# A Strassen-type factorization kernel: narrower column groups, and the sums of weight quadrants made by accumulating DMAs

## The chip, the cores and the metric

The kernel runs on one core of a Trainium2 chip. The core has five engines that run their own instruction queues side by side and meet only through semaphores: PE (matrix multiplication), DVE (vector operations), ACT (scalar engine: copies and squares here), POOL (GpSimd: elementwise additions here, and an issuer of DMAs) and SP (which only issues DMAs here). The metric is the device time of one execution in microseconds (us); lower is better.

## The reference

```python
out_lin = x @ lin_w.T + lin_b                                  # x: 1024 x 512, lin_w: 512 x 512
xv = jnp.einsum('bf,efm->bem', x, weight)                      # weight: 64 x 512 x 512
zp = jnp.einsum('bf,efm->bem', jnp.square(x), jnp.square(weight))
interaction = 0.5 * jnp.sum(jnp.square(xv) - zp, axis=1)
return out_lin + interaction
```

For each of 512 output columns m there are 64 embeddings e, so `xv` is a product of a 1024 x 512 matrix with a 512 x 32768 matrix, all in f32. Nearly all the work is there. `zp` needs no large product: summed over e it is `square(x)` times the sum over e of the squared weights, a 512 x 512 matrix called `w2_sum`.

## The kernel before, in words

**Two levels of Strassen's scheme.** The 32768 columns are done in 16 groups of 2048 (32 outputs of 64 embeddings). In each group x and the weight are cut into 2 x 2 quadrants, and seven products (outer products, numbered 1 to 7 in `ORDER = (1, 6, 2, 7, 4, 5, 3)`) stand in for eight. Each outer product is itself done in the same way, from seven inner products: that is `tree(s, g, i)` (line 416). An inner product is a "pair": two matmuls of 128 rows by 128 by 512 columns into the two banks of one PSUM buffer (`b1`, `b3`, or one of two `b2`). A group has 49 pairs, 98 matmuls; each f32 matmul shows as two records in the profile.

**The left operands.** X1 to X7, sums of quadrants of x, are built once in the beginning (lines 343 to 368), each with its seven inner sums, from x loaded into `oa0` to `oa3`.

**The right operands.** A group's weight quadrants w11, w12, w21, w22 are loaded by `load` (line 378), each in two halves of 1024 columns' worth named `.0` and `.1`. The outer sums are made in place or in T1 and T2 by `outer_sum` (line 384), all on DVE, two instructions each: T1 = w12 - w11, T2 = w22 - T1, w12 = w22 - w12, w21 = w21 - T2. The right operand of outer product i is named in `RHS` (line 412). Outer product 2 uses w21 as loaded, outer product 4 uses w21 after the last of these sums; one tree, 7, lies between them. The inner sums of each operand, `t` 1 to 4 with 512 columns, are POOL's (lines 420 to 427), in two buffers each.

**Evacuation.** Within a tree the products accumulate in PSUM: product 5 into b3, ACT copies it out as `p5`; product 3 is added into b3, ACT copies that as `p53`; product 1 into b1, ACT copies b1 into b2; 6, 7 and 4 add to b2, 2 adds to b1, and each of the four results is taken out after its product (`outer_psum` and `outer_sbuf`, lines 451 to 480) by DVE, with a second addition on DVE or POOL, into the outer results `oa`, `ob` and `c`. Finished results are squared on ACT and reduced over e on DVE (`finish`, line 402). `w_squares` does the same with the raw weights, for `w2_sum`. The buffers p5 are two, p53 three.

**The order.** All instructions are collected in a `Plan` (line 27) with costs for the engines that can do them, and `order` plays the program through on an event list: each engine takes, of what is ready, what is due first, with due times counted back from PE's sequence. Shared additions can go to DVE or POOL; DVE takes one only when it is due within 4 us (`spare`). PE's sequence itself is fixed: a product's key is 7 times the tree's number plus its place in

```python
PLACE = {5: -6, 3: -2, 1: 0, 6: 3, 2: 4, 7: 6, 4: 9}
```

so that neighbouring trees overlap: in the steady state PE runs 1, 5 of the next tree, 4 of the tree before, 6, 2, 3 of the next tree, 7, and so on. `pick` lets PE take nothing but the next product of that chain (lines 112 to 117). The order found is the static order of every engine's queue; at run time each engine waits for its semaphores in that order.

**Beginning and end.** A first stage computes `x @ lin_w.T + lin_b` (line 325) and parks it in DRAM; a last stage multiplies -0.5 square(x) by `w2_sum` (line 565), adds the parked parts and writes the output.

Of the kernel before, what the change touches and what calls it, by code (L numbers as in the profile page):

```python
# [17 lines left out]
G = 2  # L18
ORDER = (1, 6, 2, 7, 4, 5, 3)

SLOT = {1: 0, 7: 1, 2: 2, 4: 3, 5: 4, 6: 5, 3: 6}

PLACE = {5: -6, 3: -2, 1: 0, 6: 3, 2: 4, 7: 6, 4: 9}
# [3 lines left out]
class Plan:  # L27

# [33 lines left out]
    def order(self, spare=4.0):  # L62
# [6 lines left out]
        for o in reversed(ops):  # L69
            for d in o.deps:  # L70
                ops[d].succ.append(o.n)
        waiting = [len(o.succ) for o in ops]
        stack = [o for o in ops if not o.succ]
        while stack:
# [3 lines left out]
            for x in o.succ:  # L78
                latest = min(latest, ops[x].latest - cost)
# [11 lines left out]
        done, late, nxt = [], 0.0, 0  # L91
# [5 lines left out]
        def ready(o):  # L97
            return max([0.0] + [ops[d].end for d in o.deps]) + self.HOP
# [35 lines left out]
        while len(done) < len(ops):  # L134
            now = heapq.heappop(times)
            moved = True
            while moved:
                moved = False
                for e in pending:
# [6 lines left out]
                    if e == PE:  # L146
                        nxt += 1
# [25 lines left out]

@with_exitstack
def kernel(
# [8 lines left out]

    nc = tc.nc
    NG, NQ, _, NCB, KH, N = weight.shape
    B = xT.shape[1]
    M = out.shape[1]
    NB = B // P
    NK = 2 * KH
    MG = M // NG
    MI = MG // 4  # L210
    E = N // MI
    H = B // 2
    Q = B // 4

# [9 lines left out]

    buf = {}

    def make(name, shape, pool=sb):
        buf[name] = pool.tile(shape, F32, tag=name, name=name)
        return name

    def ring(tag, n, shape, pool=sb):
        names = [make(f"{tag}_{i}", shape, pool) for i in range(n)]
        state = [0]

        def take():
            state[0] += 1
            return names[(state[0] - 1) % n]
# [3 lines left out]
    half = [P, 2, N]  # L241
    for i in range(1, 8):
        make(f"X{i}", [P, 7, Q])
# [3 lines left out]
    for pos in range(4):  # L247
        make(f"oa{pos}", half)
        make(f"ob{pos}", half)
    t_ring = {k: ring(f"t{k}", 2, [P, N]) for k in range(1, 5)}  # L250
    p5_ring, p53_ring = ring("p5", 2, half), ring("p53", 3, half)
    c_ring, wsq_ring = ring("c", 3, half), ring("wsq", 2, half)
    make("b1", [P, G, N], ps)
    make("b3", [P, G, N], ps)
    b2_ring = ring("b2", 2, [P, G, N], ps)
    acc_ring = ring("acc", 2, [P, NB, MG])
    w2_sum = sb.tile([P, NK, M], F32, tag="w2_sum", name="w2_sum")
    bias = sb.tile([P, M], F32, tag="bias", name="bias_sb")
# [5 lines left out]
    PAIR = 1.72  # L264

    def two_input(o, a, b, sub, size=1024, psum=False):

        costs = {DVE: 0.08 + 1.06 * size / 1024}
        if not psum:
            costs[POOL] = 0.14 + 2.19 * size / 1024  # L270

        def emit(e):
            f = engines[e].tensor_sub if sub else engines[e].tensor_add
            f(o, a, b)  # L274

        return costs, emit

    def whole(o, a, b, sub=False, only=None, psum=False):

        costs, emit = two_input(buf[o], buf[a], buf[b], sub, psum=psum)  # L280
        plan.add({e: c for e, c in costs.items() if only in (None, e)}, emit, (a, b), (o,),
                 both=not psum)

    def act(o, i, func, reads, writes, cost=1.04):
        def emit(_):
            if func is None:
                nc.scalar.copy(o, i)  # L287
            else:
                nc.scalar.activation(o, i, func)  # L289

        plan.add({ACT: cost}, emit, reads, writes)

    def reduce(o, i, reads, writes):
        plan.add(
            {DVE: 1.14},
            lambda _: nc.vector.tensor_reduce(  # L296
                o, i.rearrange("p a (m e) -> p a m e", e=E), axis=AX.X, op=ALU.add
            ),
            reads, writes,
        )  # L300
# [3 lines left out]


    x_src = xT.rearrange("(p k) b -> p k b", k=NK)
    lw_src = lin_wT.rearrange("(p k) m -> p k m", k=NK)
    nc.gpsimd.dma_start(bias, lin_b.partition_broadcast(P))
    for k in range(NK):
        q, r = divmod(k, KH)  # L310
        for h in range(2):
            name = f"oa{2 * h + q}"
            dma(buf[name][:, r, :], x_src[:, k, ts(h, H)], (), ((name, r),),
                1.2, 2.0, nc.sync if h == 0 else nc.scalar)
        dma(buf[f"ob{q}"][:, r, :], lw_src[:, k, :], (), ((f"ob{q}", r),), 1.2, 2.0)

    lin_banks = ["b1", "b3", "b2_0", "b2_1"]
    for k in range(NK):
        q, r = divmod(k, KH)
        for g, bank in enumerate(lin_banks):  # L320
            h = g // 2

            def emit(_, k=k, q=q, r=r, g=g, h=h, bank=bank):
                for j in range(G):
                    nc.tensor.matmul(  # L325
                        buf[bank][:, j, :],
                        buf[f"oa{2 * h + q}"][:, r, ts((g * G + j) % (NB // 2), P)],
                        buf[f"ob{q}"][:, r, :],
                        start=(k == 0),
                        stop=(k == NK - 1),  # L330
                    )

            plan.add({PE: PAIR}, emit, ((f"oa{2 * h + q}", r), (f"ob{q}", r)),
                     (bank,), key=-1000 + 4 * k + g)
    for g, bank in enumerate(lin_banks):
        o = ("ob2", "ob3", "c_0", "c_1")[g]
        for j in range(G):
            costs, emit = two_input(buf[o][:, j, :], buf[bank][:, j, :], bias, False, 512, True)
            plan.add(costs, emit, (bank,), ((o, j),))
        dma(lin_dram[:, ts(g, G), :], buf[o], ((o, 0), (o, 1)), (o,))  # L340

    def block4(i):
        return buf[f"X{i}"][:, 0:4, :].rearrange("p (k q) b -> p k (q b)", k=2)

    a_buf = {"A11": "oa0", "A12": "oa1", "A21": "oa2", "A22": "oa3"}

    def a_parts(*names):
        return tuple((a_buf[n], r) for n in names if n in a_buf for r in range(KH)) + tuple(
            n for n in names if n not in a_buf
        )  # L350

    def a_ap(n):
        return buf[a_buf[n]] if n in a_buf else block4(int(n[1]))

    for i, n in ((1, "A11"), (2, "A12"), (4, "A22")):
        act(block4(i), a_ap(n), None, a_parts(n), (f"X{i}",))
    for i, a, b, sub in ((5, "A21", "A22", 0), (6, "X5", "A11", 1), (7, "A11", "A21", 1), (3, "A12", "X6", 1)):
        costs, emit = two_input(block4(i), a_ap(a), a_ap(b), sub)
        plan.add(costs, emit, a_parts(a, b), (f"X{i}",), both=True)
    for i in ORDER:  # L360
        x = buf[f"X{i}"]
        a11, a21, a12, a22 = (x[:, s, :] for s in range(4))
        s1, s2, s4 = (x[:, s, :] for s in range(4, 7))
        for o, a, b, sub in ((s1, a21, a22, 0), (s2, s1, a11, 1), (s4, a12, s2, 1), (a21, a11, a21, 1)):
            costs, emit = two_input(o, a, b, sub, 256)
            plan.add(costs, emit, (f"X{i}",), (f"X{i}",), both=True)
    for n in a_buf.values():
        plan.add({SP: 0.0}, None, (), (n,) + tuple((n, r) for r in range(KH)))
    for n in ("ob0", "ob1", "ob2", "ob3", "c_0", "c_1"):
        plan.add({SP: 0.0}, None, (), (n, (n, 0), (n, 1)))  # L370


    QUAD = ("w11", "w12", "w21", "w22")

    def w(g, q):
        return q + "ab"[g % 2] if q == "w22" else q

    def load(g):
        for q in (0, 1, 3, 2):
            for c in range(NCB):  # L380
                n = f"{w(g, QUAD[q])}.{c}"
                dma(buf[n], weight[g, q][:, c], (), (n,))

    def outer_sum(g, which):
        o, a, b = {
            1: ("T1", "w12", "w11"),
            2: ("T2", w(g, "w22"), "T1"),
            3: ("w12", w(g, "w22"), "w12"),
            4: ("w21", "w21", "T2"),
        }[which]  # L390
        for c in range(NCB):
            whole(f"{o}.{c}", f"{a}.{c}", f"{b}.{c}", True, DVE)

    def w_squares(g, q):
        row, col = divmod(QUAD.index(q), 2)
        for c in range(NCB):
            n, sq = f"{w(g, q)}.{c}", wsq_ring()
            act(buf[sq], buf[n], AF.Square, (n,), (sq,), 1.07)
            m = g * MG + (2 * col + c) * MI
            reduce(w2_sum[:, ts(row, KH), m:m + MI], buf[sq], (sq,), (("w2", row, m),))  # L400

    def finish(g, i, n, pos):
# [211 lines left out]
```

## Time and profile before

| | |
|---|---|
| median of 3 runs | 1438.88 us (1438.18 to 1439.22) |
| the profiled execution, first to last instruction | 1436.8 us |
| PE, time in matmul records | 1408.8 us, 98% |
| DVE | 1245.7 us, 87%, 1006 instructions |
| POOL | 1149.6 us, 80%, 691 instructions |
| ACT | 748.8 us, 52%, 756 instructions |
| bytes moved by DMA | 83.54 MB, a mean of 58 GB/s |

A line of the profile's groups or of its timeline names engine, source line, operation, output and inputs by the program's tile names, and the shape; `x4` is a count. "Busy" and "mean ns of one" are durations; what stands in brackets or behind a bar is the idle time of the engine just before, and who released it. PEld is the loading of the left operand into PE, which overlaps the matmul before. Most operations are recorded through one helper line, so that L274 is every addition on DVE or POOL, L287 every ACT copy, L289 every square, L296 every reduction, L438 every pair of a tree; they are told apart by tiles.

### The profile page before, as it was taken

The page shows a single profiled execution, that of the slowest core. Times are in us where ns is not written, and L with a number is a line of the kernel's source. Part 1 is how long each engine was busy: PE and PEld are TensorE (multiplying, and loading weights), DVE is VectorE, ACT ScalarE, POOL GpSimd, SP SyncE. Part 2 cuts the span into 40 slices and gives each one's busy share as a digit, 9 for nine tenths or more (in the row PEclk, how much of TensorE's full clock was granted, in tenths as well). Part 3 has the DMA queues.
Part 4 walks back from the last instruction along what each step waited for, and adds up shares of the span by engine and source line. Part 5 has one row for each costly group of instructions (what it writes and reads, how often), then busy time and mean ns, then how long its engine had stood idle before and what let it go on. Part 6 is the DMA issues. An engine that isn't in the chain of part 4 may idle for free.

```text
span 1436.8 us, 10763 instructions
## 1 busy us (share of the span) xinstructions
PE 1408.8 (98%) x3264; PEld 619.3 (43%) x3264; DVE 1245.7 (87%) x1006; ACT 748.8 (52%) x756; POOL 1149.6 (80%) x691
## 2 busy tenths in 40 slices
PE   7999999999999999999999999999999999999998
PEld 3444444444444444444444444444444444444443
DVE  1899898998989899898988989899898888989984
ACT  1465554645545465564556555465554546556441
POOL 6988886878878688896878888687887868889781
PEclk9999999999999999999999999999999999999999
DMA  5311111111111112111111111111111111210221
GB/s 212 117 60 58 48 59 33 59 48 59 59 42 51 33 59 62 46 58 33 59 48 58 59 48 59 33 59 48 58 59 45 53 32 57 60 52 22 88 74 59
DMA packets 40377, 83.54 MB, mean 58 GB/s; under 512 B 18240, under 2 KB 19264, under 8 KB 40320
## 3 DMA queue, kind: packets, MB, share of 16 engines
q1 hardware_dynamic: 39664, 81.54, 18.1%
q10 hardware_dynamic: 576, 1.05, 0.2%
q8 instruction: 27, 0.44, 0.1%
q14 instruction: 30, 0.25, 0.1%
q0 software_dynamic: 80, 0.26, 0.0%
HBM read 76.68 MB, written 6.16 MB: 58 GB/s over the span
## 4 chain that ended last, share of the span: by engine, by line
PE 90%; POOL 4%; DVE 2%; issue 1%; ACT 1%; DMA 1%; DVEq 0%; POOLq 0%; SPq 0%
PE b L438 86%; POOL oa L274 3%; PE b L325 2%; PE b L565 2%; ACT p L287 1%; POOL t L274 1%; DMA ob<-lin_wT 0%; DVE p L274 0%; DMA T1.1_83<-lind 0%; DVE ob L274 0%; DVE w11.1_73 L536 0%; DVE w21.0_76 L274 0%; DVE oa L274 0%; DVE acc L296 0%; DVE w11.0_72 L536 0%
## 5 line engine op out<-in xcount | busy, mean ns | idle before, releaser
L438 PE MATMUL b<-t,X 128*128 128x512 f32 x1792 | 806.2, 592 | 2.0 <-DVE p L274 1.6
L438 PEld LDWEIGHTS b<-t,X 128*128 128x128 f32 x1792 | 340.0, 190 | 431.9 <-issue 415.0
L287 ACT COPY p<-b 128x1024 f32<-128x1024 f32 x224 | 225.6, 1007 | 266.1 <-PE b L438 226.8
L289 ACT ACTIVATE oa<-oa 128x1024 f32<-128x1024 f32 x128 | 131.9, 1054 | 165.3 <-DVE oa L274 90.9
L296 DVE TENSOR_REDUCE w_sum<-wsq 128x16 f32<-128x1024 f32 x128 | 154.8, 1211 | 29.0 <-ACT wsq L289 28.9
L287 ACT COPY b<-b 128x1024 f32<-128x1024 f32 x112 | 111.8, 998 | 91.1 <-PE b L438 85.2
L274 DVE TENSOR_TENSOR p<-b,p 128x1024 f32<-128x1024 f32 x96 | 117.0, 1218 | 43.4 <-PE b L438 43.4
L296 DVE TENSOR_REDUCE acc<-oa 128x16 f32<-128x1024 f32 x128 | 152.0, 1207 | 0.0
L438 PE MATMUL b<-w21.0_76,X 128*128 128x512 f32 x256 | 120.3, 592 | 0.0
L274 POOL TENSOR_TENSOR oa<-oa,p 128x1024 f32<-128x1024 f32 x32 | 102.8, 3212 | 1.8
L289 ACT ACTIVATE c<-c 128x1024 f32<-128x1024 f32 x64 | 67.7, 1058 | 67.8 <-DVE c L274 67.8
L274 POOL TENSOR_TENSOR oa<-p,oa 128x1024 f32<-128x1024 f32 x32 | 75.7, 2365 | 27.2 <-DVE p L274 26.9
L274 DVE TENSOR_TENSOR oa<-b,p 128x1024 f32<-128x1024 f32 x64 | 78.0, 1219 | 11.7 <-PE b L438 10.8
L274 POOL TENSOR_TENSOR c<-c,oa 128x1024 f32<-128x1024 f32 x32 | 75.4, 2357 | 13.8 <-DVE c L274 11.7
L274 POOL TENSOR_TENSOR oa<-oa,ob 128x1024 f32<-128x1024 f32 x32 | 76.4, 2387 | 6.9 <-DVE oa L274 6.9
L274 POOL TENSOR_TENSOR ob<-ob,oa 128x1024 f32<-128x1024 f32 x32 | 76.3, 2384 | 5.5 <-DVE ob L274 5.5
L274 POOL TENSOR_TENSOR t<-w21.0_76,t 128x512 f32<-128x512 f32 x32 | 40.8, 1275 | 48.3 <-PE b L438 48.3
L274 POOL TENSOR_TENSOR ob<-p,ob 128x1024 f32<-128x1024 f32 x32 | 75.7, 2364 | 0.5 <-DVE p L274 0.5
L296 DVE TENSOR_REDUCE acc<-ob 128x16 f32<-128x1024 f32 x64 | 75.9, 1209 | 0.0
L296 DVE TENSOR_REDUCE acc<-c 128x16 f32<-128x1024 f32 x64 | 74.8, 1208 | 1.1 <-ACT c L289 1.1
L438 PEld LDWEIGHTS b<-w21.0_76,X 128*128 128x128 f32 x256 | 48.6, 190 | 61.2 <-issue 61.2
L274 DVE TENSOR_TENSOR ob<-b,oa 128x1024 f32<-128x1024 f32 x32 | 39.1, 1223 | 40.5 <-PE b L438 39.8
(127 smaller groups left out, 2295.9 us busy)
## 6 DMA issues: line engine op xcount, KB each, us to landing
w11.0_72<-weight SPq DMA_DIRECT2D x16, 512.0 KB, 3.7
w11.1_73<-weight SPq DMA_DIRECT2D x16, 512.0 KB, 3.8
w12.0_74<-weight SPq DMA_DIRECT2D x16, 512.0 KB, 3.8
w12.1_75<-weight SPq DMA_DIRECT2D x16, 512.0 KB, 3.8
w21.0_76<-weight SPq DMA_DIRECT2D x16, 512.0 KB, 3.8
w21.1_77<-weight SPq DMA_DIRECT2D x16, 512.0 KB, 4.7
w22a.0_78<-weight SPq DMA_DIRECT2D x8, 512.0 KB, 3.8
w22a.1_79<-weight SPq DMA_DIRECT2D x8, 512.0 KB, 3.8
```

Source lines behind the costliest of these rows:

```text
L274: f(o, a, b)
L287: nc.scalar.copy(o, i)
L289: nc.scalar.activation(o, i, func)
L296: lambda _: nc.vector.tensor_reduce(o, i.rearrange("p a (m e) -> p a m e", e=E), axis=AX.X, op=ALU.add),
L325: nc.tensor.matmul(buf[bank][:, j, :], buf[f"oa{2 * h + q}"][:, r, ts((g * G + j) % (NB // 2), P)], buf[f"ob{q}"][:, r, :], start=(k == 0) ...
L438: nc.tensor.matmul(buf[b][:, j, :], buf[f"X{i}"][:, SLOT[p], ts(j, P)], op, start=first, stop=True, skip_group_check=True,)
L565: nc.tensor.matmul(buf[bank][:, j, :], buf[xe[h, k // KH]][:, k % KH, ts((g * G + j) % (NB // 2), P)], w2_sum[:, k, :], start=(k == 0), st ...
```

## The change

**Groups.** The 512 outputs are done in two groups of 16 and 20 groups of 24 (1024 and 1536 columns). A matmul has 256 columns in the first two groups and 384 in the others, where it had 512; there are 22 x 98 matmuls in trees where there were 16 x 98. Each operation on PSUM or SBUF shrinks alike, from 1024 elements per partition to 512 or 768.

**Outer sums.** They become four accumulating DMAs a group, issued from POOL, each over a whole quadrant: T1 is loaded with w12 and w11 is added from DRAM; T2 is loaded with w22 and T1 is added; w22 is added to w12 and T2 to w21, both in place. Minus signs are moved to the x side (X5, X6, X7, X3). T1 has two buffers, so that there are four more load instructions a group than before: T1 and T2 are loaded too.

**Order.** PE may take any product that is ready, the one with the smallest key first, as long as it is due within 20 us (`AHEAD`); the key is a time now, and never smaller than that of a product it depends on. Dependencies are kept for pieces of 128 elements of a tile instead of whole tiles. `spare` becomes 15 us.

**Buffers.** The inner sums t of a tree share one buffer, of which there are three (there were two of each); p53 has two instead of three; `c` is one buffer of the whole result.

A second kind of tree (`wide_tree`, `widen`, `HSLOT`, `HSEQ`) is in the source as well, but `HK` is empty and none of it is executed. It is left out here.

```diff
+HK = ()
+TBUF = 3
+SPARE = 15.0
+AHEAD = 20.0
+def groups(n_m):
+    return [16, 16] + [24] * ((n_m - 32) // 24)
...
         op.deps.discard(op.n)
+        op.after = max((self.ops[d].after for d in op.deps), default=-1e9)
+        if key is not None:
+            op.key = op.after = max(key, op.after + 1e-6)
...
-                if nxt < len(chain):
-                    o = chain[nxt]
-                    if not left[o.n] and ready(o) <= now + 1e-6:
-                        return o
-                return None
+                able = [n for n in pending[e]
+                        if ops[n].latest < now - late + AHEAD and ready(ops[n]) <= now + 1e-6]
+                return ops[min(able, key=lambda n: ops[n].key)] if able else None
...
-    for q in ("w11", "w12", "w21", "w22a", "w22b", "T1", "T2"):
-        for c in range(NCB):
-            make(f"{q}.{c}", half)
+    for q in ("w11", "w12", "w21", "w22a", "w22b", "T1a", "T1b", "T2"):
+        make(q, KH * WIDE)
...
-    p5_ring, p53_ring = ring("p5", 2, half), ring("p53", 3, half)
+    t_ring = ring([make(f"t{k}", 12 * V) for k in range(TBUF)])
+    p5_ring = ring([make(f"p5_{k}", WIDE) for k in range(2)])
+    p53_ring = ring([make(f"p53_{k}", WIDE) for k in range(2)])
...
+    def dma_add(o, i, rows, reads, writes):
+        token = ("token", len(plan.ops))
+        def emit(_):
+            nc.gpsimd.dma_start(o, i, accum_op=ALU.add)
+        cost = 2.9 * rows / 1024
+        plan.add({POOL: 1.0}, emit, reads + writes, writes + (token,), land=cost + 2.5)
+        plan.add({SP: cost}, None, (token,), ())
...
-    for i, a, b, sub in ((5, "A21", "A22", 0), (6, "X5", "A11", 1), (7, "A11", "A21", 1), (3, "A12", "X6", 1)):
+    tt(x_block(5), x_in(1, 1), x_in(1, 0), True)
+    minus_both(x_block(6), x_block(5), x_in(0, 0))
+    tt(x_block(7), x_in(0, 0), x_in(1, 0), True)
+    minus_both(x_block(3), x_in(0, 1), x_block(6))
...
     def outer_sum(g, which):
-        o, a, b = {
-            1: ("T1", "w12", "w11"),
-            2: ("T2", w(g, "w22"), "T1"),
-            3: ("w12", w(g, "w22"), "w12"),
-            4: ("w21", "w21", "T2"),
+        o, i = {
+            1: (w(g, "T1"), None), 2: ("T2", w(g, "T1")), 3: ("w12", w(g, "w22")), 4: ("w21", "T2"),
         }[which]
-        for c in range(NCB):
-            whole(f"{o}.{c}", f"{a}.{c}", f"{b}.{c}", True, DVE)
+        n = KH * GROUPS[g] // 2 * E
+        o = reg(o, 0, n)
+        if i is None:
+            dma_add(o.ap, source(g, 0), n, (), o.atoms)
+        else:
+            dma_add(o.ap, reg(i, 0, n).ap, n, reg(i, 0, n).atoms, o.atoms)
...
-            plan.add({PE: PAIR}, emit, (name, f"X{i}", b), (b,), key=7 * s + PLACE[p])
+        pair = 2 * mm_cost(n)
+        def product(p, bank, first):
+            mm([reg(bank, j * N, n) for j in range(2)],
+               [reg(f"X{i}", SLOT[p] * Q + j * P, P) for j in range(2)],
+               rhs[p], first, time + PLACE[p] * pair)
...
-        load(g)
+        load(g, (("w11", 0), ("w12", 1), (w(g, "T1"), 1), ("T2", 3)))
         outer_sum(g, 1)
         outer_sum(g, 2)
+        load(g, ((w(g, "w22"), 3), ("w21", 2)))
         w_squares(g, "w12")
```

The function `minus_both(o, a, b)` writes -a - b and runs on DVE only; `reg` names a piece of a tile; `source(g, q)` is the part of the weight in DRAM that belongs to quadrant q of group g.

More of the change, by code (lines that the diff above doesn't have):

```diff
@@ L90, in order @@
         times = [self.HOP]
[L91 removed]
+        done, late = [], 0.0
         def release(o):
@@ L97, in ready @@
         def ready(o):
-            return max([0.0] + [ops[d].end for d in o.deps]) + self.HOP
+            return max([0.0] + [d.end for d in o.waits]) + self.HOP
         def longer(e, by):
@@ L171, in order, with __init__, ap @@
         return done
+class Reg:
+    def __init__(self, tile, off, n, *outer):
+        self.tile, self.off, self.n, self.outer = tile, off, n, outer
+        self.size = n
+        offs = [off]
+        for step, count in outer:
+            self.size *= count
+            offs = [o + step * k for o in offs for k in range(count)]
+        unit = tile.unit
+        self.atoms = tuple(sorted({
+            (tile.name, a) for o in offs for a in range(o // unit, (o + n - 1) // unit + 1)
+        }))
+    @property
+    def ap(self):
+        t = self.tile.ap
+        free = [list(x) for x in self.outer] + [[1, self.n]]
+        return bass.AP(tensor=t.tensor, offset=t.offset + self.off, ap=[list(t.ap[0])] + free)
 @with_exitstack
@@ L272, in emit @@
         def emit(e):
             f = engines[e].tensor_sub if sub else engines[e].tensor_add
[L274 to L284, printed above, removed]
+            f(o.ap, a.ap, b.ap)
+        plan.add({e: c for e, c in costs.items() if only in (None, e)}, emit,
+                 a.atoms + b.atoms, o.atoms, both=not psum)
@@ L337 @@
[L337 to L349, printed above, removed]
-        )
@@ L352, in a_ap @@
[L352 to L356, printed above, removed]
-    for i, a, b, sub in ((5, "A21", "A22", 0), (6, "X5", "A11", 1), (7, "A11", "A21", 1), (3, "A12", "X6", 1)):
-        costs, emit = two_input(block4(i), a_ap(a), a_ap(b), sub)
-        plan.add(costs, emit, a_parts(a, b), (f"X{i}",), both=True)
+        name, off = ("c", g * 2 * M) if g < 3 else ("w22b", 0)
@@ new lines, with source, load @@
+    base = [0]
+    for mg in GROUPS:
+        base.append(base[-1] + mg)
+    def source(g, q):
+        iw = GROUPS[g] // 2 * E
+        lo = base[g] * F * E + q * P * KH * iw
+        return weight[lo:lo + P * KH * iw].rearrange("(p x) -> p x", p=P)
+    def load(g, names):
+        iw = GROUPS[g] // 2 * E
+        for name, q in names:
+            for k in range(KH):
+                o = reg(name, k * iw, iw)
+                dma(o.ap, source(g, q)[:, k * iw:(k + 1) * iw], (), o.atoms, 2.4 * iw / 1024)
```

552 lines of the change are left out of this document (362 added, 190 removed).

## The prediction

> **What bounds the kernel now.** I read the page first, for how full each engine is.
>
> ```profile
> span 1436.8 us, 10763 instructions
> PE 1408.8 (98%) x3264; PEld 619.3 (43%) x3264; DVE 1245.7 (87%) x1006; ACT 748.8 (52%) x756; POOL 1149.6 (80%) x691
> PEclk9999999999999999999999999999999999999999
> L438 PEld LDWEIGHTS b<-t,X 128*128 128x128 f32 x1792 | 340.0, 190 | 431.9 <-issue 415.0
> ```
>
> The PE is the bound, at full clock; no other engine is. What can be won is what the PE loses, so next comes its ideal pitch, from the timeline of the last stage, where nothing makes it wait, and of the cold start:
>
> ```profile
> 8.88 0.34 PEld L325 LDWEIGHTS b<-ob,oa 128*128 128x128 f32 x1 [0.52 <-issue]
> 13.15 0.28 PEld L325 LDWEIGHTS b<-ob,oa 128*128 128x128 f32 x1 [0.52 <-issue]
> ...
> 1404.47 1.88 PE L565 MATMUL b<-w_sum,w11.0_72 128*128 128x512 f32 x4
> ...
> 1430.22 1.88 PE L565 MATMUL b<-w_sum,w12.1_75 128*128 128x512 f32 x4
> ```
>
> Between the last two rows start 15 times 4 = 60 matmul records: 25.75/60 = 0.4292 us each (one matmul of the code is two records, a "product" on two halves is four). Cold, five records take 4.27 us, 0.854 each; half of that is 0.427, so some 0.0022 us a record doesn't shrink with the clock. The chain of waits gives the rest:
>
> ```profile
> 7.90 30.40 PE b L325 x64
> ...
> 288.04 3.30 POOL oa L274
> 291.38 0.94 issue
> 292.32 1.00 ACT p L287
> ...
> 373.24 3.29 POOL oa L274
> ...
> 1432.14 0.69 DVE w22a.1_79 L274
> ```
>
> A group repeats every 373.24-288.04 = 85.20 us; its 196 records need 196 x 0.4292 = 84.12. So 1.08 us a group is lost, 17.3 in 16 groups. The whole: 1432.14-7.90 = 1424.2, less 3264 x 0.4292 = 1400.9, less 30.40 - 64 x 0.4292 = 2.9 for the cold clock, leaves 20.4 us: 17.3 at the group turns, some 3 at the first and the last tree. The list of waits names the place, and the timeline at one turn the cause:
>
> ```profile
> PE b L438 <- ACT p L287: 13.4, 16, 1.1
> PE b L438 <- DVE p L274: 1.6, 2, 1.4
> ```
>
> ```profile
> 114.74 1.78 DVE L274 TENSOR_TENSOR T1.0_82<-w12.0_74,w11.0_72 128x1024 f32<-128x1024 f32 x1
> 116.44 2.28 DVE L274 TENSOR_TENSOR ob<-ob,p 128x1024 f32<-128x1024 f32 x1
> 117.60 3.33 POOL L274 TENSOR_TENSOR oa<-oa,p 128x1024 f32<-128x1024 f32 x1
> 118.64 3.36 DVE L274 TENSOR_TENSOR T2.0_84<-w22b.0_80,T1.0_82 128x1024 f32<-128x1024 f32 x1
> 121.92 0.99 ACT L287 COPY p<-b 128x1024 f32<-128x1024 f32 x1
> 122.97 1.55 PE L438 MATMUL b<-w11.1_73,X 128*128 128x512 f32 x3 [0.83 <-ACT p L287]
> ```
>
> DVE's outer sums T1 and T2 of the next group run side by side with POOL's last use of the buffer p of tree 5; both stretch (3.33 us, where the rows below have 2.37 for that size). p comes free late, the copy into it is late, product 3 of tree 1 waits.
>
> **The change part by part.** The instructions get shorter. These rows give two sizes for each kind, or one:
>
> ```profile
> L274 DVE TENSOR_TENSOR T2.0_84<-b,w21.0_76 x2: 677/678/680, 1412.0 to 1412.6; 128x512 f32<-128x512 f32 x2
> ```
>
> ```profile
> L274 DVE TENSOR_TENSOR p<-b,p 128x1024 f32<-128x1024 f32 x96 | 117.0, 1218 | 43.4 <-PE b L438 43.4
> L287 ACT COPY p<-b 128x1024 f32<-128x1024 f32 x224 | 225.6, 1007 | 266.1 <-PE b L438 226.8
> L274 POOL TENSOR_TENSOR oa<-p,oa 128x1024 f32<-128x1024 f32 x32 | 75.7, 2365 | 27.2 <-DVE p L274 26.9 <-POOL t L274 0.3
> L274 POOL TENSOR_TENSOR t<-w21.0_76,t 128x512 f32<-128x512 f32 x32 | 40.8, 1275 | 48.3 <-PE b L438 48.3
> ```
>
> *Columns.* Two groups with matmuls of 256 columns and 20 with 384 stream the same 1,605,632 columns as 16 x 196 records of 512, in 22 x 196 = 4312 records, 1176 more. At 0.0022 us that is +2.6 us; the lower bound is 0 (all of the pitch goes with the columns). Above: the weight load of 190 ns lies under a record of 216 ns at 256 columns and of 322 at 384, so hidden; were it a pitch of 0.23, the 392 small records would cost 5.5 us more. I take 2.6. A product takes 4 x 0.3222 = 1.29 us in a large group, 0.863 in a small one.
>
> *Outer sums off DVE.* DVE loses 8 instructions a group (T1.0 1.78, T2.0 3.36, w21.0 2.02 below among them), and with them the jam at the turn: -17.3. Linear between the rows, a 768-element DVE operation takes 0.95 us, POOL's 1.82, POOL's 384 sum 1.00. A large group has 63.1 us of PE work; DVE has 28 evacuations and 24 reductions, 52 x 0.95 = 49; POOL 28 sums t, 28, up to 14 shared additions, 25, and four DMA issues, which the nearest row puts at 0.68 each, 3: 56. Both fit, and DVE may take shared additions from POOL. So the ordinary windows should hold: the pair of products that hides an evacuation lasts 2.58 us against 0.2 (159.12 to 159.32 below) + 0.95 + 0.05 (the copy's end at 122.91 to 122.97) = 1.20.
>
> *What is late next.* The addition of T2 to w21 must come after tree 2 has used the raw w21 and before tree 4's first sum t. Before, that looks so:
>
> ```profile
> 149.58 1.22 DVE L274 TENSOR_TENSOR w21.1_77<-w21.1_77,T2.1_85 128x1024 f32<-128x1024 f32 x1
> ...
> 157.41 1.88 PE L438 MATMUL b<-w21.0_76,X 128*128 128x512 f32 x4
> 159.12 1.88 PE L438 MATMUL b<-w12.1_75,X 128*128 128x512 f32 x4
> 159.32 1.22 DVE L274 TENSOR_TENSOR oa<-b,oa 128x1024 f32<-128x1024 f32 x1 [0.42 <-PE b L438]
> 160.47 2.02 DVE L274 TENSOR_TENSOR w21.0_76<-w21.0_76,T2.0_84 128x1024 f32<-128x1024 f32 x1
> ...
> 162.57 1.28 POOL L274 TENSOR_TENSOR t<-w21.1_77,w21.0_76 128x512 f32<-128x512 f32 x1 [1.16 <-DVE w21.0_76 L274]
> ...
> 164.27 4.03 PE L438 MATMUL b<-t,X 128*128 128x512 f32 x9
> ```
>
> One half was added early, the other after product 2 (streamed until 159.12), and product 5 of tree 4 began 5.15 us later, just in time: three products lie between. In the changed kernel one accumulating DMA adds all of w21 after that product 2, and three products are 3.87 us. How long it takes is not in the trace; the nearest rows are plain transfers:
>
> ```profile
> 1.25 0.68 POOL L308 DMA_DIRECT2D bias_sb<-lin_b  x1 [0.80 <-POOLq L603]
> ```
>
> ```profile
> w11.0_72<-weight SPq DMA_DIRECT2D x16, 512.0 KB, 3.7
> accd<-acc SPq DMA_DIRECT2D x15, 128.0 KB, 2.4
> ```
>
> 1.3 us for 384 KB more gives 2.0 + 2.6 = 4.6 us for 768 KB, the lower bound; if every byte is handled twice (source and old destination), 2.0 + 5.2 = 7.2; two whole transfers in a row, 9.2, are the upper bound. I take 6, between the first two. Product 5 is then ready 0.2 (to POOL) + 0.5 (half of a POOL sum in the way) + 6 + 0.1 + 1.0 (t) + 0.1 = 7.9 us after product 2. Until then the new order lets PE go on: 3, 7, 1, 4, 6, 2, 7 of trees 2 and 7 are free, 7 x 1.29 = 9.03 us; the eighth, product 4 of tree 7, must wait for the evacuation ahead of it. So the DMA is hidden, with 1.1 us to spare. It costs nonetheless: with tree 4 left out, one product instead of two covers each evacuation, 1.29 against 1.20, and any DVE operation in the way shows. I allow a third of one, 0.3 us in each of 20 groups, 6 us (bounds 0 and 0.95 x 20 = 19). In the small groups the same count gives 6.2 against 6.04 us, and 0.93 against 0.863 for each evacuation: 1 us each, 2.
>
> *The rest.* Four more loads a group and the other three accumulations have 15 us and more between free and due (T2 is free after the addition to w21, three trees before the turn, and due a tree later); behind a DMA that waits on POOL's queue stand sums t and shared additions, and the third t buffer covers a tree, 9 us. Preparing X is due sooner, since small trees take 6.0 us, and now has two steps for DVE alone. All x has landed here:
>
> ```profile
> 18.51 1.04 ACT L287 COPY X<-oa 128x1024 f32<-128x1024 f32 x1 [5.47 <-DMA oa<-xT]
> ```
>
> From there to the first product (7.90 + 30.40 = 38.3) are 20 us; 28 steps of 256 columns at 0.41 (the DVE line) and four of 1024 at 1.22 are 16.4 on DVE alone, which no longer has T1 and T2 there: 0, and a few us if that cover fails. The last stage can fill the last tree's 1.4 us wait: -1.
>
> Sum against the profiled execution: 1436.8 - 17.3 + 2.6 + 6 + 2 - 1 = 1429.1; the median of the runs lies 2.1 above that execution's span: **1431 us**.
>
> **Rivals.** *The accumulation is late (slower).* Place: product 5 of tree 4, once a group. Each us over 9.03 - 1.9 = 7.1 is paid 20 times; it outweighs the gain from about 7.5 us a DMA (0.39 x 20 = the 7.7 us won). At 8.2, between the two upper bounds, 1.07 x 20 = 21.4, and 1 more in each small group: 1429.1 + 21.4 + 2 + 2.1 = 1455; at 9.2, 1477. For it: the source and destination must both be read, and the whole addition sits in one DMA. Against: few bytes are on the way,
>
> ```profile
> q1 hardware_dynamic: 39664, 81.54, 18.1%
> ```
>
> and nothing else becomes free to load at that point.
>
> The Trainium skill (TensorE: Matmul & The Clock Gate, "Why this matters for your kernels") says that PE gaps of over about 3 us bring the half clock back. The cold rows above show that clock, and no wait in this trace is long enough to show its return; by that rule a DMA of over 10 us would cost up to 2.9 us more a group, as the cold start did.
>
> *POOL can't issue in time (slower).* The turn above shows DVE and POOL stretching each other; if an issue is held up likewise, by a two-input DVE operation of 2.3 us, product 5 is ready at 10.2, 1.2 late: 1429.1 + 24 + 2.1 = 1455 as well. Against: without outer sums few DVE operations have both inputs in SBUF. The Trainium skill (SBUF — State Buffer, "Who interferes with whom") describes POOL-issued DMAs starved of descriptors by DVE, but for DVE's two-port modes, and infers that two-input additions don't do it; no run here shows an accumulating issue.
>
> *The wait only moves (no change).* With 0.7 instead of 0.3 us a group lost behind single covers, 1431 + 8 = 1439. For it: slack of 0.09 us; against: DVE has 20% left.
>
> *Nothing waits.* Without the 8 us allowed, 1423. Against: the same 0.09.
>
> **How the numbers follow.** Forecast 0.42 (own range 1424 to 1436); nothing waits 0.10; the wait moves 0.12; the accumulation late 0.28; the issue late 0.08. About 0.2% (2.9 us) is what a measurement can tell from no change: faster 0.52, same 0.12, slower 0.36. Range: from 1421, the forecast without any lost time and without the extra records, to 1465, which takes in the late cases up to a DMA of 8.7 us.
>
> **What would show it.** Right: no wait of product 3 on a copy at the turn; no T1, T2 sums on DVE; w21's accumulation landing within 7 us and PE running through it; groups repeating every 63.1 to 63.7 us. Wrong: PE waiting on POOL's t of tree 4; a POOL DMA issue of over 2 us; records of 256 columns apart by more than 0.22 us; new waits on DVE evacuations of over 0.7 us a group.

## The result, and the profile after

| | before | after |
|---|---|---|
| median | 1438.66 us (16 runs, 1438.18 to 1439.22) | 1442.9 us (16 runs, 1436.66 to 1447.37) |
| ratio to before, 95% interval | | 1.0029 [1.0016, 1.0042] |
| profiled execution | 1436.8 us | 1444.8 us |

The changed kernel is slower by 0.3%, where faster by 0.5% was forecast. What stands out besides is the spread: 1 us before, 10.7 us after. The page of the changed kernel, busy times:

```profile
PE 1422.6 (98%) x4440; PEld 839.8 (58%) x4440; DVE 1101.6 (76%) x1226; ACT 786.4 (54%) x1038; POOL 1149.3 (80%) x995
```

DVE has lost 144 us, as planned, and PE is still the bound. Where it loses time, the chain of waits of the changed kernel tells (start, duration, what):

```profile
6.12 26.97 PE b L369 x56
...
34.41 5.15 DVE X L391
...
102.59 7.95 DMA w<-T
...
117.75 8.50 DMA T<-T1a
...
168.28 60.94 PE b L335 x188
...
230.18 0.94 DVE acc L314
231.12 0.87 DVE oa L289
232.04 60.94 PE b L335 x188
...
701.01 5.91 DVE ob L289
...
1320.00 84.42 PE b L335 x260
...
1407.86 5.16 PE b L335 x16
...
1416.45 1.29 PE b L335 x4
...
1421.17 1.29 PE b L335 x4
```

Four places can be read off. **Regular groups** repeat every 232.04 - 168.28 = 63.76 us; 196 records at 0.3225 us (the twelve that start between 217.41 and 221.28 us) are 63.21, so 0.55 us is lost in each, 11 us in 20. **One event**: from 168.28 to 1320.00 are 18 periods, 1147.7 us, and 4.0 us more; they lie around 701. **The start**: 18 x 196 records and the last 284 leave 500 of 4312 ahead of 168.28, 392 of 256 columns (0.2158 us each) and 108 of 384: 119.4 us. The first stage's 64 records, begun at 6.12, take 64 x 0.4292 and 2.9 us more for the cold clock, and end at 36.5; 131.8 us were taken from there, so 12.4 us are lost before the groups become regular. **The end** loses 0.6 us: 284 x 0.3225 + 64 x 0.4292 = 119.1 of the 119.7 us from 1320.00 to the end of the last matmul at 1439.67.

The timeline of the changed kernel in two of these places, the start and the second narrow group:

```profile
25.77 0.88 POOL L325 DMA_DIRECT2D T<-T1a  x1 [2.13 <-DMA T1a<-weight]
...
34.33 5.24 DVE L391 SCALAR_TENSOR_TENSOR X<-oa,X 128x1024 f32<-128x1024 f32 x1
...
110.68 2.05 PE L335 MATMUL b<-w,X 128*128 128x256 f32 x4 [2.04 <-DMA w<-T]
```

At 25.77 POOL's queue had stood still for 2.13 us behind an accumulation that waits for T1a. All that POOL had to do then came in one gapless stretch, and the addition for X3 on DVE, whose two inputs are both in SBUF, took 5.24 us, where it takes 1.74 in E3 below. At 110.68 the accumulation into w21 was late itself, and the product after the gap took 2.05 us in place of 1.03.

The event around 701 us, with the same place one group later below it:

```profile
684.10 0.86 POOL L325 DMA_DIRECT2D T<-T1b  x1 [0.95 <-DMA T<-weight]
...
700.38 1.92 POOL L289 TENSOR_TENSOR oa<-oa,p 128x768 f32<-128x768 f32 x1
...
701.01 5.90 DVE L289 TENSOR_TENSOR ob<-ob,p 128x768 f32<-128x768 f32 x1
702.15 1.11 POOL L289 TENSOR_TENSOR t<-w,t 128x384 f32<-128x384 f32 x1
...
703.10 1.10 POOL L289 TENSOR_TENSOR t<-T,t 128x384 f32<-128x384 f32 x1
...
704.06 1.09 POOL L289 TENSOR_TENSOR t<-T 128x384 f32<-128x384 f32 x1
...
705.01 1.08 POOL L289 TENSOR_TENSOR t<-w,t 128x384 f32<-128x384 f32 x1
...
707.86 2.93 PE L335 MATMUL b<-w,X 128*128 128x384 f32 x4 [2.17 <-ACT p L299]
...
768.26 1.81 POOL L289 TENSOR_TENSOR oa<-oa,p 128x768 f32<-128x768 f32 x1 [0.27 <-DVE p L289]
...
768.89 2.00 DVE L289 TENSOR_TENSOR ob<-ob,p 128x768 f32<-128x768 f32 x1
...
770.03 1.72 POOL L289 TENSOR_TENSOR t<-w,t 128x384 f32<-128x384 f32 x1
```

A load of T came late (5.8 us from issue to landing, 4.4 one group later), POOL stood 0.95 us behind the accumulation that waits for it, and from there on POOL has no time to spare: its instructions overlap, the next starts 0.14 us and more before the one ahead has ended (702.15 against 700.38 + 1.92). DVE's addition, dispatched in the midst of them, ends only after POOL has run dry at 706.1. Then p is late, the copy is late, PE waits 2.17 us. One group later POOL isn't pressed: its next instruction starts only 0.04 us before the end of the one ahead (770.03 against 768.26 + 1.81), DVE gets in after that one, and the POOL instruction is the one that waits (1.72). In the other regular groups POOL waited at this place for 0 to 0.53 us, and the addition took 2.0 us.

And what the prediction asked first, how long an accumulation takes (kilobytes each, median us from issue to landing, changed kernel):

```profile
w<-T POOLq DMA_DIRECT2D x20, 768.0 KB, 6.0
...
T1a<-weight POOLq DMA_DIRECT2D x10, 768.0 KB, 7.0
...
T1b<-weight POOLq DMA_DIRECT2D x10, 768.0 KB, 8.5
```

### The profile page after: what moved, and what is told of

Same layout as the page of the kernel before. It is cut to its first block, busy times and chain, and to the rows that moved or that the text cites. A ratio compares the mean times of both kernels' runs of the same rounds, so it can differ in the third digit from the quotient of the medians.

```text
span 1444.8 us, 14609 instructions
## 1 busy us (share of the span) xinstructions
PE 1422.6 (98%) x4440; PEld 839.8 (58%) x4440; DVE 1101.6 (76%) x1226; ACT 786.4 (54%) x1038; POOL 1149.3 (80%) x995
## 4 chain that ended last, share of the span: by engine, by line
PE 91%; DVE 4%; issue 2%; DMA 1%; POOL 1%; ACT 0%; DVEq 0%; SPq 0%; POOLq 0%; ACTq 0%
PE b L335 87%; PE b L776 2%; PE b L369 2%; DVE oa L289 1%; DVE acc L314 1%; DVE ob L289 1%; DMA T<-T1a 1%; DMA w<-T 1%; POOL t L289 0%; DVE c L289 0%; DVE X L391 0%; DMA ob<-lin_wT 0%; DVE p L289 0%; ACT p L299 0%; POOL w L325 0%
## 5 line engine op out<-in xcount | busy, mean ns | idle before, releaser
L335 PE MATMUL b<-t,X 128*128 128x384 f32 (+1 forms) x2464 | 825.9, 478 | 2.7 <-ACT p L299 1.3
L335 PEld LDWEIGHTS b<-t,X 128*128 128x128 f32 x2464 | 464.7, 190 | 317.5 <-POOL t L289 11.8
L299 ACT COPY p<-b 128x768 f32<-128x768 f32 (+1 forms) x308 | 239.2, 777 | 329.7 <-PE b L335 306.2
L335 PE MATMUL b<-w,X 128*128 128x384 f32 (+1 forms) x1056 | 370.8, 481 | 6.2 <-ACT p L299 2.2
L335 PEld LDWEIGHTS b<-w,X 128*128 128x128 f32 x1056 | 199.7, 191 | 143.8 <-DVE oa L289 16.5
L289 POOL TENSOR_TENSOR t<-w 128x384 f32<-128x384 f32 (+1 forms) x176 | 173.1, 996 | 35.6 <-PE b L335 32.9
L289 POOL TENSOR_TENSOR t<-w,t 128x384 f32<-128x384 f32 (+1 forms) x176 | 188.1, 1069 | 9.6 <-PE b L335 8.5
L305 ACT ACTIVATE oa<-oa 128x768 f32<-128x768 f32 (+1 forms) x176 | 140.4, 822 | 70.3 <-POOL oa L289 38.4
L314 DVE TENSOR_REDUCE w_sum<-wsq 128x12 f32<-128x768 f32 (+1 forms) x176 | 160.2, 921 | 17.8 <-ACT wsq L305 16.3
L314 DVE TENSOR_REDUCE acc<-oa 128x12 f32<-128x768 f32 (+1 forms) x176 | 158.2, 919 | 0.5 <-ACT oa L305 0.5
```

What stands on the lines that cost most here:

```text
L289: f(o.ap, a.ap, b.ap)
L299: nc.scalar.copy(o.ap, i.ap)
L305: lambda _: nc.scalar.activation(o.ap, i.ap, AF.Square), i.atoms, o.atoms)
L314: nc.vector.tensor_reduce(o, x, axis=AX.X, op=ALU.add)
L335: nc.tensor.matmul(a.ap, b.ap, w.ap, start=start, stop=True, skip_group_check=True)
```

## The experiments

Theory A, from these readings: the accumulations themselves are quick enough, but they stand in POOL's queue; where one waits for a load, POOL falls behind, and a two-input DVE addition is kept from its turn. Besides, tree 4 left out of the overlap costs 0.55 us a group. Rivals: the DMAs as such, the narrow columns, the new order, the narrow groups. One thing holds for all experiments: `order` is run anew for each, so an edit also brings another order of all queues and another split of the shared additions (POOL has 995 instructions in the changed kernel, 914 in E2, 850 in E3, 938 in E5). A difference between two runs is that of the edit together with the order that it brings. Each ratio is to the kernel before, measured beside it.

**E1: narrow groups at the end.**

```diff
-    return [16, 16] + [24] * ((n_m - 32) // 24)
+    return [24] * ((n_m - 32) // 24) + [16, 16]
```

> Only the list of groups is turned: twenty of 24 outputs first, the two of 16 at the end. Theory A (most of the excess over the forecast, some 10 us, is lost while the narrow groups meet the preparation of X and late accumulating DMAs at the start): the first trees take 9 us instead of 6, some 8 us come back, and 1 to 2 us are paid at the end: about 1436 us. Rival B (the accumulating DMAs or the regular groups cost it): no change, 1441 to 1445 us.

Measured 1440.29 us (1436.86 to 1445.91), ratio 1.0014 [1.0001, 1.0026]. Between the two: the start's losses stay, at other places (a wait behind the addition to w21 of the first group, X3's addition held for 4.7 us), and so does the spread (9 us). That the groups are narrow is not the point. And the event of 701 us has a second instance here, with a wait as long as there (timeline of E1):

```profile
207.00 0.86 POOL L325 DMA_DIRECT2D T<-T1b  x1 [1.03 <-DMA T<-weight]
...
223.83 5.97 DVE L289 TENSOR_TENSOR ob<-ob,p 128x768 f32<-128x768 f32 x1
```

**E2: outer sums back on DVE.**

```diff
...
-            dma_add(o.ap, reg(i, 0, n).ap, n, reg(i, 0, n).atoms, o.atoms)
...
+        for k in range(KH):
+            tt(reg(o, k * n, n), reg(a, k * n, n), reg(b, k * n, n), False, DVE)
...
-        load(g, (("w11", 0), ("w12", 1), (w(g, "T1"), 1), ("T2", 3)))
+        load(g, (("w11", 0), ("w12", 1), (w(g, "w22"), 3), ("w21", 2)))
...
```

> The outer sums go back to DVE (two instructions of 768 elements each, pluses kept), T1 and T2 are no longer loaded; groups, buffers and order stay. Theory A: DVE gets 8 instructions of 0.95 us or more a group, the meeting with POOL at the turn comes back for about 1 us in each of 20 groups, and the late accumulations at the start go: 1450 to 1460 us. Rival B (the accumulating DMAs cost more than they free): faster than the changed kernel, 1430 to 1438 us.

Measured 1443.11 us (1442.5 to 1443.93), ratio 1.0032 [1.002, 1.0043]: neither. The page shows the price on DVE:

```profile
PE 1418.2 (98%) x4440; PEld 838.5 (58%) x4440; DVE 1301.7 (90%) x1395; ACT 785.7 (55%) x1038; POOL 1191.3 (83%) x914
```

In this frame the sums cost as much on DVE, at 90%, as by DMA; but with them on DVE the spread is 1.4 us. The spread thus comes with the DMAs. The loss in the regular groups is what theory A expected (three groups take 192.8 us, from 485.80 to 678.61 in the chain of waits, 1.06 us a group over the records); the total is below its range, and the start, counted as above, loses 4.9 us in place of 12.4.

**E3: no additions.** In `outer_sum` nothing is emitted.

> All four accumulating DMAs are left out (T1 and T2 are only loaded, w12 and w21 stay as loaded), so the outer sums are missing from the result. Theory A: the regular loss of 0.6 us a group shrinks since tree 4 needs no wait, the start gains some 4 us, the preparation of X still costs: 1425 to 1434 us. Rival B' (columns and records alone make the kernel slower, whatever the sums cost): 1440 us or more.

Measured 1422.16 us (1421.89 to 1422.42), ratio 0.9885 [0.9872, 0.9899]. Faster than expected: the start loses little, and the regular groups have no wait at all (chain of waits of E3):

```profile
36.30 17.67 PE b L335 x80
...
123.07 1248.15 PE b L335 x3872
```

1248.15/3872 = 0.3224. The start, counted as for the changed kernel (6.38 for the first transfer, 27.5 and 2.9 for the first stage, 119.4 for the first 500 records of trees, which are done at 158.4), loses 2.3 us, against 12.4 there. So narrow columns, narrow groups, the free order and the preparation of X cost little; 20.7 us hang on the four accumulations and on what the order makes of them. X3's addition takes 1.74 us here.

**E4: PE's order fixed.**

```diff
...
-                return ops[min(able, key=lambda n: ops[n].key)] if able else None
+                o = chain[sum(c.end is not None for c in chain)] if any(c.end is None for c in chain) else None
+                ok = o is not None and not left[o.n] and ready(o) <= now + 1e-6
+                return o if ok else None
```

> PE's sequence is fixed by the keys again, nothing is taken ahead; all else as in the changed kernel. Theory A: product 5 of tree 4 is ready some 8 us after product 2 of tree 2 and three products last 3.9 us, so 4 us and more are lost in each of 20 groups, and gaps of that length bring the slow clock back: 1525 to 1560 us. Rival C (the free order does nothing here): 1441 to 1447 us.

Measured 1569.28 us, ratio 1.0907 [1.0892, 1.0922], 9 us above the expected range, with the wait where it was expected (waits of E4, total us, times, longest):

```profile
PE b L335 <- POOL t L289: 90.2, 23, 6.3
```

They are 3.9 us each, and the granted clock falls to 0.966 in the mean. The free order is worth 126 us here, and without it the accumulation into w21 would not have been hidden.

**E5: the addition to w21 in two halves**, by inner rows; the first half has b11 and b12, of which tree 4's first sum is made, and is free four products earlier.

```diff
-            dma_add(o.ap, reg(i, 0, n).ap, n, reg(i, 0, n).atoms, o.atoms)
+            for k in range(KH if which == 4 else 1):
+                h = n // KH if which == 4 else n
+                q, s = reg(o.tile.name, k * h, h), reg(i, k * h, h)
+                dma_add(q.ap, s.ap, h, s.atoms, q.atoms)
```

> Only the addition of T2 to w21 is cut into two DMAs, by the two rows of inner blocks; the first half holds all that tree 4's first sum t needs and is free four products earlier. Theory A (the 0.6 us lost in each large group is the gap that tree 4's lateness leaves in the overlap of trees): the groups repeat every 63.2 instead of 63.76 us, 20 x 0.55 = 11 us less, about 1432 us, with a spread as wide as the changed kernel's. Rival D (the 0.6 us come from load on DVE and POOL as such): no change, 1441 to 1445 us.

Measured 1445.41 us (1442.29 to 1446.53), ratio 1.0044 [1.0032, 1.0057]: no gain. But the 0.55 us have gone from where they were; a new wait has taken their place (waits, and the timeline of one group, of E5):

```profile
POOL T1a L325 <- DMA T1a<-weight: 16.8, 9, 2.7
POOL T1b L325 <- DMA T1b<-weight: 15.9, 9, 2.7
```

```profile
639.40 0.87 POOL L325 DMA_DIRECT2D T1b<-weight  x1 [1.72 <-DMA T1b<-weight]
640.01 2.12 POOL L289 TENSOR_TENSOR oa<-oa,p 128x768 f32<-128x768 f32 x1
...
642.16 0.80 ACT L299 COPY p<-b 128x768 f32<-128x768 f32 x1 [3.70 <-POOL oa L289]
...
643.01 1.24 PE L335 MATMUL b<-w,X 128*128 128x384 f32 x3 [0.22 <-ACT p L299]
```

The instruction order that the plan found for the halves puts the accumulation into T1b ahead of oa<-oa,p, and POOL stands 1.72 us before it until the load has landed: 5.0 us after its issue, where the plan reckons 2.4 x 768/1024 + 1.5 = 3.3. Behind it stands the addition that frees p: the jam at the turn of the groups, which DVE's sums made before, made now by a DMA.

**E6: loads planned to land later.**

```diff
-                dma(o.ap, source(g, q)[:, k * iw:(k + 1) * iw], (), o.atoms, 2.4 * iw / 1024)
+                dma(o.ap, source(g, q)[:, k * iw:(k + 1) * iw], (), o.atoms, 2.4 * iw / 1024, 3.5)
```

> Only the plan's landing time of the weight loads is 3.5 instead of 1.5 us, so that POOL's queue comes to an accumulating DMA later. Theory A (now and then a load of T lands 1 us late, POOL's queue stands behind the DMA that waits for it, POOL has a backlog, and DVE's addition with two SBUF inputs gets no turn for 6 us): the spread of 10 us between executions shrinks to under 4 us and the median falls by 3 to 6 us, to 1437 to 1440 us. Rival E (the spread comes from something else, such as the DMAs' own duration): spread of 8 us or more, median unchanged.

Measured 1497.67 us (1497.43 to 1497.91), ratio 1.0412 [1.0398, 1.0426]. The spread shrank as expected (0.5 us), the median rose by 55 us against the forecast of a fall: groups repeat every 66.77 us. One instruction a group tells why; first its row in the changed kernel, below it that in E6:

```profile
L289 DVE TENSOR_TENSOR ob<-ob,p 128x768 f32<-128x768 f32 x19 | 41.8, 2199 | 0.0
```

```profile
L289 DVE TENSOR_TENSOR ob<-ob,p 128x768 f32<-128x768 f32 x19 | 119.1, 6267 | 0.0
```

What befell one group in the changed kernel befalls all here: POOL is in the midst of a stretch of overlapping instructions each time DVE comes to ob<-ob,p. That addition takes 4.1 us more, of which 3.0 show in the time of a group. But the start of it is another than at 701 (timeline of E6):

```profile
181.28 0.84 POOL L325 DMA_DIRECT2D w<-w22b  x1
...
181.87 1.28 POOL L289 TENSOR_TENSOR t<-T 128x384 f32<-128x384 f32 x1
...
187.36 2.04 POOL L289 TENSOR_TENSOR oa<-oa,p 128x768 f32<-128x768 f32 x1
...
187.75 6.26 DVE L289 TENSOR_TENSOR ob<-ob,p 128x768 f32<-128x768 f32 x1
...
189.12 1.23 POOL L289 TENSOR_TENSOR t<-w,t 128x384 f32<-128x384 f32 x1
```

POOL waits for no load here, in this group or in any regular one. The overlap begins with the issue of an accumulating DMA in a queue without a pause (181.87 against 181.28 + 0.84), and it lasts as long as POOL has no pause. The transfer itself isn't what holds DVE: it had landed at 187.48, before the addition began, and no other accumulation was under way until 205.6. So a late load is one way into the jam, and an issue at an unlucky place of the order is another.

**E7 and E11: halves and late loads together**, E7 with the narrow groups last besides.

> The addition to w21 in halves, the loads planned late and the narrow groups at the end, together. Theory A: 11 + 4 + 2 us less than the changed kernel, 1424 to 1429 us, faster than the kernel before, with a spread under 4 us. If only one of the three readings is right: 1431 to 1440 us.

> The addition to w21 in halves and the loads planned late, with the narrow groups first as in the changed kernel. Theory A (the halves' own gain of some 11 us was eaten by POOL waiting for T1's loads, which planning them late removes; the narrow groups first cost 2 to 4 us more than last): 1430 to 1434 us. Rival H (most of the gain of the three together came from the narrow groups last): 1438 us or more.

E7: 1429.48 us (1428.7 to 1429.7), ratio 0.9937 [0.9924, 0.9951], at the upper end of what was expected. E11: 1428.52 us (1427.66 to 1429.05), ratio 0.9931 [0.9918, 0.9943], below its range, because the place of the narrow groups is again worth nothing. Each edit alone gained nothing or lost; together they make a kernel that is faster than the kernel before and the changed one, with a spread of 1.4 us. In E11 PE has no wait in the regular groups (chain of waits of E11):

```profile
105.65 1257.74 PE b L335 x3932
```

No POOL wait on a T1 load is left there but one in the first group. POOL also has less to do, 74% in place of 80%, since the order found gives DVE more of the shared additions; the runs don't separate the two. What E11 still lacks against E3, 6.4 us, is lost for the most part in the first two groups: the 389th record of a tree begins at 123.07 in E3 and 5.1 us later, at 128.15, in E11; some 1 us is lost at the end.

**E8: the kernel before without outer sums**, T1 and T2 only loaded.

> The kernel before with its outer sums left out: T1 and T2 are loaded from DRAM with w12 and w22, w12 and w21 stay as loaded, so these sums are missing from the result. Theory A (DVE's outer sums make the wait at each turn): the 1.08 us a group go, 1419 to 1424 us. Rival F (the wait at the turn comes from POOL's last use of p alone): 1435 us or more.

Measured 1426.53 us (1426.07 to 1427.32), ratio 0.9918 [0.9904, 0.9931]. Between the two: 12 us, not 17.3 (chain of waits of E8):

```profile
112.76 77.53 PE b L439 x180
...
190.32 1.22 DVE c L274
...
197.24 77.53 PE b L439 x180
```

A group still takes 84.48 us, 0.36 more than its records: of the 1.08 us at the turn the sums made two thirds. The rest stands behind a row of DVE operations that begins at 190.32.

**E9, E10 and E12: second additions on POOL alone**, no two-input addition on DVE in the trees; E9 on top of E6, E10 on the changed kernel, E12 on E7.

```diff
-                    tt(part(o, pos), part(o, pos), small(p))
+                    tt(part(o, pos), part(o, pos), small(p), False, POOL)
...
-                tt(o, z, a)
+                tt(o, z, a, False, POOL)
```

> The kernel of the loads planned late, with the second additions of the evacuations (two SBUF inputs) on POOL alone, none on DVE. There DVE's ob<-ob,p took 6.3 us in the mean where the changed kernel's takes 2.2. Theory A (POOL's gapless queue keeps DVE's two-input addition from its turn, and that alone makes the 55 us): 1436 to 1450 us. Rival G (the late additions to T and T1 or the other order make the 55 us): 1480 us or more.

> The changed kernel with only that edit: the second additions on POOL alone. Theory A (the 10 us of spread are single groups in which DVE's addition is kept waiting): spread under 4 us, no group with a wait of over 2 us in it, median 1436 to 1440 us, unless POOL, with 2 additions a group more, falls behind. Rival E (the spread has another source): spread of 8 us and more.

> The three edits together (1429.5 us) and the second additions on POOL alone. Theory A: the 7.5 us that DVE's c<-c,oa took in the first group go, 4 us less, 1424 to 1428 us, unless POOL's load (28 sums and 14 additions a group, some 56 of 63 us) makes its sums late: then 1430 to 1436 us.

E9: 1455.37 us, ratio 1.0113 [1.0099, 1.0127]. 42 of the 55 us of E6 are gone with the DVE addition; the expected range is missed by 5, and since the edit has a price of its own (E10), it isn't shown that the addition made all 55. E10: 1449.52 us (1448.79 to 1451.12), ratio 1.0077 [1.0063, 1.0091]: the spread falls from 10.7 to 2.3 us, as theory A had it; the median doesn't fall to its 1436 to 1440 us, since each group takes 0.34 us longer (chain of waits of E10):

```profile
577.38 35.13 PE b L335 x108
...
641.48 35.13 PE b L335 x108
```

The period is 64.10 us. E12: 1434.26 us, ratio 0.9967 [0.9955, 0.998], 4.8 us worse than E7, in the range that was given for a late POOL. So the DVE additions, beside accumulating DMAs, make the spread, but POOL, at 83 to 86% with them, cannot take them for nothing. What helped in these runs was an order in which POOL neither waits for a load nor is pressed when DVE adds in the regular groups (E7, E11), not more work for POOL.

## Why the prediction was wrong, point by point

**The jam at the turn, -17.3.** Right in kind, too large: E8 gives 12.0. The last third of the 1.08 us has another cause, a row of DVE operations in E8's chain of waits.

**Columns, +2.6.** Right as far as it can be seen: 0.3225 and 0.2158 us a record against 0.3222 and 0.863/4 = 0.2158, no sign of the weight load showing, and E3's regular groups run at that pitch.

**The accumulation into w21, hidden.** Right: 6.0 us, as taken, with PE running through it, and E4 shows what the order is worth. The 6 was picked between two bounds, so that the exact hit is in part luck; the other accumulations took 6.0 to 8.5. The 0.3 us allowed for single covers were 0.55 (231.12 in the chain: an evacuation behind a reduction), 11 us in place of 6. E5 and E11 confirm the mechanism: once the first half comes early, the wait is gone.

**"The rest", put at 0.** This is the step that failed. It argued with the data: the other three accumulations have 15 us between free and due, and a third t buffer covers POOL. In the regular groups no wait of PE on these sums shows, but the slack does not help: what is late is not the sum but what stands behind its DMA in POOL's queue, and what DVE does beside it. The t buffers cover the sums t; they do not cover the additions that free p (E5), nor DVE's two-input additions, which are held while POOL's instructions overlap (the event at 701, X3 at 34.33, each group of E6). The first groups lost 12.4 us, where 2 were allowed for the narrow ones and 0 for the preparation of X; without accumulations (E3) they lose 2.3, so the 2 was about right and some 10 us belong to the 0. A single group lost 4 us more in the profiled execution, and one in that of E1. How many such groups an execution has would fit the spread of 10.7 us, but only one execution of each kernel was profiled, so that is not shown. Preparing X was hardly a cost of its own (E3); it became one behind the first accumulation, which POOL came to 2.13 us before its load had landed.

None of the signs that the prediction named for being wrong showed: PE waited 0.4 us in all on a sum t, no issue took over 1.4 us, the narrow records are 0.2158 us apart, and DVE's evacuations cost 0.55 us a group. They look at PE in the regular groups; none looks at POOL's queue or at the start.

**The rivals.** "The accumulation is late" put the lateness at product 5 of tree 4; it was seen once in the changed kernel, in a narrow group, at a product that reads w21 itself (110.68). "POOL can't issue in time" was the nearest in kind, with POOL and DVE in each other's way, but had the wrong victim: not the issue, which took 0.87 us, but DVE's addition and POOL's own. "The wait only moves" came nearest in number, with 1439 us from 0.7 us a group; the regular groups lose 0.55, but it has nothing of the start and the event. None foresaw that the price is paid in POOL's queue, behind a DMA that waits there or is issued there without a pause.

**The sum.** The forecast of 1429.1 has 10 us of lost time in it: 6 in the regular groups, 2 in the narrow ones, and 2 left of the 3 at the first and the last tree. Measured are 28: 11 in the regular groups, 12.4 at the start, 4.0 in the event, 0.6 at the end. With 18 more, and 1.8 less because the first transfer landed sooner (6.12 in place of 7.90), 1445.3 comes out, against 1444.8.

Not tried: why a load of T lands 1 us late in single groups. The runs show what follows from it, not where it comes from. Nor was one order kept while only the DMAs changed, so what belongs to an edit and what to its new order is shown only where a trace tells it.

## What to carry to other kernels

When work moves to DMAs that a compute engine issues, ask of each such DMA what it waits for, what stands behind it in that engine's queue, and what another engine does beside it; slack between free and due says nothing about that. Cut a transfer so that the piece that is due first goes alone, and compare the landing times that the plan reckons with those of the trace; but look at the order that comes of it, for late landing alone cost 55 us here (E6). Where a change gains nothing, look whether its gain has turned into a new wait: here two edits that gained nothing one by one made a kernel 1% faster than the changed one together.

## What the runs showed of the hardware

**DVE's two-input addition can be passed over by several POOL instructions in a row.** At 768 elements ob<-ob,p took 2.0 us where POOL's next instruction overlapped the one ahead by 0.04 us (770.03), and 5.9 to 6.3 us where each overlapped by 0.14 to 0.30 us (701.01; E1; E6). Overlaps of over 0.1 us come with accumulating DMAs on POOL: the traces have none in the whole of the kernel before, E2, E3 and E8, which have no such DMA, and 73 to 606 in each of the others. The Trainium skill (SBUF — State Buffer, "Who interferes with whom") calls the pair of ports that DVE and GpSimd share an exclusive lock, says that a DVE instruction with two SBUF inputs contends with a GpSimd instruction that reads SBUF, and lets the order of issue decide who blocks. The 2.00 and 1.72 us at 769 agree with that; in a stretch of overlapping instructions the runs show the same side getting it again, four times in a row.

**PE's clock fell after shorter gaps than expected.** The windows of the two gaps and of what follows them in the changed kernel (window, length, PE busy, granted clock, share of the DMA engines, GB/s):

```profile
108.64:110.68 2.04, 0.00 (x2) 0.96 0.72 199
110.68:112.73 2.05, 2.05 (x5) 0.50 0.58 150
...
705.60:707.80 2.20, 0.09 (x1) 1.00 0.42 87
707.86:710.79 2.93, 2.93 (x5) 0.50 0.15 60
```

After 2.04 and 2.17 us without a matmul the next product ran at a clock of 0.50, 2.05 us in place of 1.03 and 2.93 in place of 1.45. The Trainium skill (TensorE: Matmul & The Clock Gate, "Why this matters for your kernels") gives gaps of over about 3 us; here 2 us were enough, twice. They aren't always: in E6 some twenty waits of up to 1.8 us left the granted clock at 1.000, and in E9 one of 2.35 us at 1380.8 did not bring the half clock.

**An accumulating DMA** of 768 KB took 6.0 to 8.5 us at the median in the changed kernel, its issue 0.8 to 0.9 us of POOL's time in all but four of 88; plain loads of half the size took 3.4 to 5.2 us.
